# Two graph-attention layers on one core: how an aggregate's products end, and how a column of numbers becomes a row

## The chip, the cores and the metric

The kernel runs on one core of a Trainium2 chip. The core has TensorE (PE in the profile; PEld are its weight loads), VectorE (DVE), ScalarE (ACT), GpSimd (POOL) and SyncE (SP), and 16 DMA engines that move data between HBM and the on-chip memory. TensorE writes its products to PSUM, which has eight banks; DVE or ACT must copy a result out of a bank before another product may start there. The metric is the device time of one execution in microseconds (us); the times below are medians over several executions.

## The reference

There are 2708 nodes with 1024 features (`x`) and a 0/1 adjacency matrix `adj` of 2708 x 2708; all is fp32. Two layers follow each other, each with a layer norm and relu ahead of it and a residual around it:

```
h = maximum(layernorm(x), 0)                     # layer 0
f = h @ Wf + bf ;  g = h @ Wg + bg
e = relu(f @ g.T)
A = softmax(where(adj > 0, e, -9e15), axis=1)
x = x + A @ (h @ W + bW)

h = maximum(layernorm(x), 0)                     # layer 1
z = h @ W1 ;  f1 = z @ a1 ;  f2 = z @ a2
e = leaky_relu(f1 + f2.T, 0.2)
A = softmax(where(adj > 0, e, -9e15), axis=1)
x = x + relu(A @ z)
```

## The kernel before

**Tiling.** The 2708 rows are cut into 21 full tiles of 128 rows and one, TINY, of 20. Twenty full tiles form five panels (`p` = 0 to 4) and ten pairs (`pairs`, `NQ` = 10). The 21st tile (MONO) and TINY are the leftover unit: their columns are spread over panels 0 to 2, so that the panels are 576, 576, 532, 512 and 512 columns wide. Scores are held transposed: a panel is a block of columns (the rows of the reference's `A`), and all 22 tiles run through it.

**Stages.** A first phase, whose later tiles run between the score products of panel 0, normalizes `x`, transposes it, multiplies the weights `Wf` and `Wg` together and writes to DRAM what the later stages stream: `hs_d` for the scores, `hg_d` and `hgl_d` (pairs and leftovers) for the aggregates, `mk_d` for the masks. It also fills `r_`, the part of the scores that depends on one node alone; `r_` lies with 128 nodes down the partitions and a tile per column. In layer 0 each panel then goes through `scores` (score products, masks, running maximum), `column_max` and `softmax` (exponentials and their sum), `aggregate` (attention times `h`) and `project` (times `W`). Layer 1 computes its scores from two vectors (`weights1`), and goes through `aggregate` and `project` again. The stages of neighbouring panels are interleaved in the main loop (L1358 to L1387): `aggregate` of panel `p` comes after `project_q` of panel `p+1`, and `project` of panel `p` comes ahead of the scores of panel `p+1`, but for the last two panels, where the order differs. After panel 0's aggregate, background work that is left is run down (`flush`), and `spread_wa` follows.

**Strassen-Winograd.** Each large product is done with seven half-size products M1 to M7 instead of eight. `accumulate` (L554 to L585) runs them in a given order. A product accumulates over `K` steps into `NH` = 4 banks. With `by_k` set (the aggregates), the loop over the ten pairs is outside and that over the four banks inside, so that all four banks end together. M1 and M2 share the banks called x, M5 and M3 those called y, M6 and M7 those called z; M4 has its own, v. There are eight banks in all: z takes x's banks after M2, and the small products after M3 (`sum_ps`, `mx_ps`) take y's. In the profile a bank's name follows the aggregate: `gx`, `gy`, `gz`, `gv`.

**The end of a product in `aggregate`** (L788 to L880). The order is M1, M5, M2, M6, M3, M7, M4. `left` (L815) loads the left operands (`hc`, 512 KB for two pairs) when they are first asked for. M2, M3 and M4 also take in the leftover unit: `left_over` (L822) loads `hl` and multiplies MONO (L828) and then the 20 rows of TINY (L832) into the same four banks. It is called as `more[m]` after the last pair; after it come the four evictions (`evict`, L860) and one call of `behind`. M7 computes another leftover product at its middle pair (`into_m15`, banks `gw`). M2's eviction is a copy by ACT into `gT`, M3's an addition by DVE into `gT`.

**What sets the order of work.** Each engine runs its instructions in order. SP issues all loads in program order (`load`, L137), POOL issues the stores (`store`, L141), which a scheduler may move. Streamed operands share one pool of 12 buffers (`strm`), so a load can wait until an older buffer is free. `behind` runs background jobs (exponentials, masks, weight preparation) between TensorE's products at a given rate; in an aggregate it is called after pairs 2, 5 and 8 and at the end.

**From a column to a row.** The scores need `r` of a panel as a row on all partitions (`rb`). `spread` (L229) transposes one column after another on TensorE, up to four into one bank, and copies the banks out, by DVE and ACT in turn. `scores` (L1055) calls it at its start in each panel. Layer 1 spreads its own vectors in the same way. DVE and ACT instructions all carry line L45, that of a helper which records them.

Of the kernel before, what the change touches and what calls it, by code (L numbers as in the profile page):

```python
# [8 lines left out]
FP = mybir.dt.float32  # L9
# [9 lines left out]
P = 128  # L19
W = 512  # L20
# [37 lines left out]
def kernel(  # L58
# [19 lines left out]
    nc = InOrder(tc)  # L78
    N, D = x.shape
    NC = D // P  # L80
    NH = NC // 2
# [3 lines left out]
    NP = N // W  # L85
# [3 lines left out]
    width = [W + NM, W + NM, W + NY, W, W]  # L89
    base = [sum(width[:p]) for p in range(NP)]  # L90
    F = W // P
    MONO, TINY = F * NP, F * NP + 1
# [9 lines left out]
    pieces = [[(t, P) for t in full(p)] + ([(MONO, NM), (MONO, NM), (TINY, NY)][p:p + 1] if p < 3 else [])  # L102
              for p in range(NP)]
    first_col = [sum(len(q) for q in pieces[:p]) for p in range(NP)]
# [55 lines left out]
    md_d = dram.tile([P, 7, NH, W], FP, name="md_d")  # L160
    wt_d = [dram.tile([P, 4, NH, W], FP, name=f"wt{l}_d") for l in range(2)]
    mk_d = [dram.tile([P, NQ + 1, 2, width[p]], BF, name=f"mk_d{p}") for p in range(NP)]
    x1_d = [dram.tile([P if t < TINY else NY, D], FP, name=f"x1_d{t}") for t in range(NT)]

    ident = consts.tile([P, P], FP, name="ident")
# [31 lines left out]
    def behind(us, psum_free=False):  # L197
        credit[0] = min(credit[0] + us, 2 * us)
        while later and credit[0] > 0 and (psum_free or not later[0][3]) and (not later[0][4] or later[0][4]()):
            credit[0] -= one()  # L200

    def flush():
        while later:
            one()
# [24 lines left out]
    def spread(o, cols):  # L229

        at = 0
        for g in range(0, len(cols), 4):
            ps = bank("sp_ps")
            w = 0
            for cl in cols[g:g + 4]:
                n = cl.shape[0]
                nc.tensor.transpose(ps[:, w:w + n], cl.to_broadcast([n, P]), ident[:n, :n])
                w += n
            copy(o[:, at:at + w], ps[:, :w])
            at += w  # L240

    def add(o, a, b):
        nc.vector.tensor_tensor(o, a, b, OP.add)
# [4 lines left out]
    def columns_of(p, col):  # L248
        return [col[:n, i:i + 1] for i, (_, n) in enumerate(pieces[p])]
# [301 lines left out]
        picks.append(t)  # L551


    def accumulate(left, right, K, h, order, then, evict, name, prepare={}, rate=0.0, by_k=False, more={}, room=()):  # L554

        acc = {}
        at = {M1: "x", M2: "x", M5: "y", M3: "y", M6: "z", M7: "z", M4: "v" if by_k else "z"}
        for m in order:  # L560
            start = at[m] not in acc
            if start:
                acc[at[m]] = [bank(f"{name}{at[m]}{d}") for d in range(NH)]
            ps = [t[:, :h] for t in acc[at[m]]]
            for k, d in ([(k, d) for k in range(K) for d in range(NH)] if by_k else
                         [(k, d) for d in range(NH) for k in range(K)]):
                nc.tensor.matmul(ps[d], left(m, k, d), right(m, k), start=(start and k == 0),  # L567
                                 stop=(k == K - 1 and m not in more), skip_group_check=True)
                if by_k and d == NH - 1 and k % 3 == 2:
                    behind(rate)  # L570
                if by_k and d == NH - 1 and k == K // 2 and (m, k) in more:
                    more[m, k]()
                if not by_k and k == K - 1:
                    evict[m](d, ps[d])
                    behind(rate, m in room)
            if by_k:
                if m in more:
                    more[m](ps)
                for d in range(NH):
                    evict[m](d, ps[d])  # L580
                behind(rate)
            if m in prepare:
                prepare[m]()
            if m in then:
                then[m]()  # L585
# [202 lines left out]
    def aggregate(l, p, S, sm, then={}, rate=3.0):  # L788


        w = width[p]
        h = w // 2
        lo, hi = slice(0, h), slice(h, w)
        T1 = [slot("T1", (P, 2, HX)) for _ in range((NQ + 1) // 2)]
        t1 = lambda q: T1[q // 2][:, q % 2, :h]
        wa_ = lambda q: S[pairs[q][0]]
        wb_ = lambda q: S[pairs[q][1]]
        exps_until(NQ)
        for q in range(NQ):
            sub(t1(q), wa_(q)[:, hi], wa_(q)[:, lo])  # L800

        def second():
            exps_until(2 * NQ + 2 + LAG)
            for q in range(NQ):
                sub(wa_(q)[:, hi], wb_(q)[:, hi], wa_(q)[:, hi])
            for q in range(NQ):
                sub(wa_(q)[:, lo], wb_(q)[:, hi], t1(q))

        def fourth():
            for q in range(NQ):  # L810
                sub(wb_(q)[:, lo], wb_(q)[:, lo], wa_(q)[:, lo])

        hc = {}

        def left(m, q, d):  # L815
            i, j = group_of[q]
            if (m, i) not in hc:
                hc[m, i] = stream("hc", (P, 2, W))
                load(hc[m, i], hg_d[l][i][:, m])
            return hc[m, i][:, j, d * P:(d + 1) * P]  # L820

        def left_over(ps, e, s, start=False):  # L822


            two = stream("hl", (P, W + P))
            load(two, hgl_d[l][:, e])
            for d in range(NH):
                nc.tensor.matmul(ps[d], two[:, d * P:(d + 1) * P], S[MONO][:, s], start=start, stop=False,  # L828
                                 skip_group_check=True)
            for d in range(NH):  # L830
                g = slice(B32 * d, B32 * d + NY)
                nc.tensor.matmul(ps[d], two[g, W:], S[TINY][g, s], start=False, stop=True, skip_group_check=True)  # L832

        def into_m15():
            ps = [bank(f"gw{d}")[:, :h] for d in range(NH)]
            left_over(ps, 1, hi, True)
            for d in range(NH):
                add(get("m15", d), ps[d], get("m15", d))

        def right(m, q):  # L840
            if m == M5:
                return t1(q)
            s = wa_(q) if m in (M1, M6, M7) else wb_(q)
            return s[:, hi if m in (M3, M7) else lo]

        G = [None, None]
        tmp = {}
        part = lambda t, d: t[d // 2][:, d % 2, :h]

        def g(e, d, s):  # L850
            if G[0] is None:
                G[:] = both("gT")
            return G[e].rearrange("p (c i) -> p c i", c=NH)[:, d, s]

        def get(name, d):
            if name not in tmp:
                tmp[name] = in_pairs(name)
            return part(tmp[name], d)

        evict = {M1: lambda d, ps: nc.scalar.copy(get("m1", d), ps),  # L860
                 M5: lambda d, ps: add(get("m15", d), ps, get("m1", d)),
                 M2: lambda d, ps: nc.scalar.copy(g(0, d, lo), ps),
                 M6: lambda d, ps: add(get("u2", d), ps, get("m1", d)),
                 M3: lambda d, ps: add(g(0, d, hi), ps, get("u2", d)),
                 M7: lambda d, ps: (add(g(1, d, hi), ps, get("m15", d)), add(get("m1", d), ps, get("m1", d))),
                 M4: lambda d, ps: add(g(1, d, lo), ps, get("m1", d))}
        inverse = []
        of = lambda e, s: G[e].rearrange("p (c i) -> p c i", c=NH)[:, :, s]
        by = lambda s, k: inverse[0][:, s].rearrange("p (o i) -> p o i", o=1).to_broadcast([P, NH, k])

        def scale():
            for e, s, k in ((0, slice(0, w), w), (1, hi, h)):
                nc.gpsimd.tensor_tensor(of(e, s), of(e, s), by(s, k), OP.mult)  # L873

        accumulate(left, right, NQ, h, (M1, M5, M2, M6, M3, M7, M4), then, evict, "g",
                   {M5: second, M2: fourth, M3: lambda: inverse.append(inverse_sums(p, sm)), M7: scale}, rate=rate,
                   by_k=True, more={M2: lambda ps: left_over(ps, 0, lo), M3: lambda ps: left_over(ps, 0, hi),
                                    M4: lambda ps: left_over(ps, 1, lo), (M7, NQ // 2): into_m15})
        nc.vector.tensor_tensor(of(1, lo), of(1, lo), by(lo, h), OP.mult)
        return [t.rearrange("p (c i) -> p c i", c=NH) for t in G]  # L880
# [148 lines left out]
    def spread_wa():  # L1029
        for k in range(2):  # L1030
            spread(wab[k], [wa[:, k, c:c + 1] for c in range(NC)])
# [23 lines left out]
    def scores(p, B):  # L1055
# [3 lines left out]
        lo, hi = slice(0, h), slice(h, w)  # L1059
        fetch, convert, turn = makers[p]  # L1060
        rb = slot("rb")
        spread(rb, columns_of(p, r_[:, first_col[p]:]))
        acc = slot("acc")
        S = [None] * NT
        rates = (0.6, 1.0, 0.65, 0.65, 0.65)
# [294 lines left out]
    for p in range(NP):  # L1360
# [17 lines left out]
        G[p] = aggregate(0, p, S, got["sm"], then)  # L1378
        if p == 0:
            flush()  # L1380
            spread_wa()
        if p < NP - 2:
            project(0, p, G.pop(p), finish0(p), {M1: lambda p=p: first_masks(p + 1, 0),
# [126 lines left out]
```

## Time and profile before

| | |
|---|---|
| median of 4 runs | 3137.21 us (3135.26 to 3141.41) |
| the profiled execution | 3141.41 us |
| its span (first to last instruction) | 3139.3 us |
| mean granted TensorE clock | 0.989 |
| TensorE busy | 3050.6 us, 97% |
| DVE / ACT / POOL busy | 58% / 14% / 15% |
| the chain that ended last | PE 89%, DVE 4%, DMA 3% |
| data moved | 651.82 MB, 208 GB/s in the mean |

The page and the answers of the trace describe one execution. A row of the timeline or of the chain gives start (us from the start of the span), duration in us, engine, line of the kernel, the names of result and operands, and the number of instructions in the row; brackets give idle time ahead of it and what ended it. A row of the waits gives, after the colon, the total in us, the number of waits and the longest. One fp32 product appears as two instructions. `<-` stands between a result and its operands.

### The profile page before, as it was taken

Reading aid. Unit: us, or ns where it says so; the run is one execution under the profiler, and the core shown is the slowest. Engines: PE = TensorE matmul, PEld = TensorE weight load, DVE = VectorE, ACT = ScalarE, POOL = GpSimd, SP = SyncE. Lnnn points to the kernel's source line nnn. Section 1 sums busy time; section 2 is a strip of 40 time slices with the busy share of each in tenths; the row PEclk is TensorE's granted clock in tenths of the full one; section 3 lists DMA queues with packets and bytes.
Section 4 is the critical chain, followed back from the end, with each engine's and each line's share of the span. In section 5 each row is a group of like instructions: output and inputs, shape, how many; then the busy total and the mean of one; then the engine's idle time right before and its main releaser. Section 6 shows DMA issues by size and latency. Waiting matters only on the chain.

```text
span 3139.3 us, 36230 instructions
## 1 busy us (share of the span) xinstructions
PE 3050.6 (97%) x12712; PEld 2263.6 (72%) x12712; DVE 1828.6 (58%) x3730; ACT 447.2 (14%) x788; POOL 464.9 (15%) x668
## 2 busy tenths in 40 slices
PE   8978999999999999999999999998999999999998
PEld 4566777767877588876888885865757758678684
DVE  5877686286732687327872478659473571745612
ACT  3321020000200101000020002103031130311200
POOL 2653002210002110023000101021010020120202
PEclk9989999999999999999999999998999999999999
DMA  6888938878446796468955678596555565565655
GB/s 209 310 281 269 270 125 305 231 229 246 154 134 161 221 256 209 147 151 259 291 174 151 170 218 246 191 294 241 192 183 170 158 200 159 167 197 171 215 163 190
DMA packets 379109, 651.82 MB, mean 208 GB/s; under 512 B 170848, under 2 KB 211328, under 8 KB 378928
## 3 DMA queue, kind: packets, MB, share of 16 engines
q1 hardware_dynamic: 335920, 525.38, 55.4%
q0 software_dynamic: 43008, 124.13, 11.8%
q8 instruction: 101, 1.65, 0.2%
q14 instruction: 80, 0.66, 0.1%
HBM read 536.68 MB, written 112.67 MB: 207 GB/s over the span
## 4 chain that ended last, share of the span: by engine, by line
PE 89%; DVE 4%; DMA 3%; issue 1%; SPq 1%; POOL 1%; ACT 0%; DVEq 0%; POOLq 0%; ACTq 0%
PE gz L567 12%; PE gy L567 12%; PE gx L567 11%; PE sz L1077 7%; PE gv L567 6%; PE pz L969 6%; PE sx L1077 5%; PE sy L1077 5%; PE px L969 4%; PE py L969 4%; PE qz L567 3%; PE qy L567 2%; PE M_ps L483 2%; PE qx L567 2%; SPq L139 1%
## 5 line engine op out<-in xcount | busy, mean ns | idle before, releaser
L1077 PE MATMUL sz<-B,As 128*128 128x288 f32 (+2 forms) x1200 | 292.3, 393 | 8.2 <-DVE st L45 7.5
L1077 PEld LDWEIGHTS sz<-B,As 128*128 128x128 f32 x1200 | 227.4, 190 | 58.1 <-DVE st L45 11.9
L873 POOL TENSOR_TENSOR gT<-gT,rr 128x2304 f32<-128x2304 f32 (+5 forms) x20 | 72.7, 3637 | 1103.1 <-DVE rr L45 1000.0
L1077 PE MATMUL sx<-B,As 128*128 128x288 f32 (+2 forms) x800 | 201.5, 395 | 13.1 <-DMA As<-hs_d 12.2
L1077 PE MATMUL sy<-B,As 128*128 128x288 f32 (+2 forms) x800 | 199.0, 392 | 0.0
L567 PE MATMUL gz<-P,hc 128*128 128x288 f32 (+2 forms) x800 | 186.0, 393 | 2.3 <-ACT gT L45 2.3
L567 PE MATMUL gz<-Sa,hc 128*128 128x288 f32 (+2 forms) x800 | 186.0, 393 | 2.3 <-ACT gT L45 2.3
L567 PE MATMUL gx<-P,hc 128*128 128x288 f32 (+2 forms) x800 | 186.8, 395 | 0.1
L1077 PEld LDWEIGHTS sx<-B,As 128*128 128x128 f32 x800 | 152.4, 191 | 44.9 <-DMA As<-hs_d 12.7
L567 PE MATMUL gy<-T,hc 128*128 128x288 f32 (+2 forms) x800 | 184.2, 391 | 0.0
L567 PEld LDWEIGHTS gx<-P,hc 128*128 128x128 f32 x800 | 153.5, 192 | 33.2 <-issue 1.9
L567 PEld LDWEIGHTS gz<-Sa,hc 128*128 128x128 f32 x800 | 151.2, 190 | 36.0 <-ACT gT L45 4.4
L567 PEld LDWEIGHTS gz<-P,hc 128*128 128x128 f32 x800 | 150.9, 190 | 35.7 <-ACT gT L45 4.5
L567 PEld LDWEIGHTS gy<-T,hc 128*128 128x128 f32 x800 | 152.0, 190 | 30.5
L1077 PEld LDWEIGHTS sy<-B,As 128*128 128x128 f32 x800 | 151.7, 190 | 30.6 <-DVE st L45 0.3
L969 PE MATMUL pz<-w,ps 128*128 128x512 f32 x320 | 142.1, 594 | 0.8 <-DVE pt L45 0.8
L969 PE MATMUL py<-w,ps 128*128 128x512 f32 x320 | 142.2, 594 | 0.0
L969 PE MATMUL px<-w,gT 128*128 128x512 f32 x320 | 141.8, 595 | 0.0
L143 POOL DMA_DIRECT2D out_dram<-x_res x180 | 89.2, 502 | 265.0 <-DVE x_res L45 242.6
L45 DVE TENSOR_TENSOR gT<-gy,u 128x288 f32<-128x288 f32 (+2 forms) x40 | 14.8, 432 | 183.5 <-PE gy L832 183.5
L45 DVE TENSOR_TENSOR u<-gz,m 128x288 f32<-128x288 f32 (+2 forms) x40 | 17.6, 440 | 170.9 <-PE gz L567 170.5
L143 POOL DMA_DIRECT2D mk_d<-mask x55 | 36.0, 655 | 541.4 <-DVE mask L45 518.2
(318 smaller groups left out, 5092.3 us busy)
## 6 DMA issues: line engine op xcount, KB each, us to landing
hc<-hg_d SPq DMA_DIRECT2D x350, 512.0 KB, 3.9
As<-hs_d SPq DMA_DIRECT2D x150, 512.0 KB, 5.4
w<-wt_d SPq DMA_DIRECT2D x96, 512.0 KB, 5.2
w<-in_L_gnn_W_dram SPq DMA_DIRECT2D x72, 512.0 KB, 4.1
md<-md_d SPq DMA_DIRECT2D x56, 512.0 KB, 4.4
adj_i<-in_adj_dram SPq DMA_DIRECT2D x200, 128.0 KB, 4.8
hs_d<-hsT POOLq DMA_DIRECT2D x40, 512.0 KB, 4.7
hg_d<-g POOLq DMA_DIRECT2D x36, 512.0 KB, 5.0
```

The costliest lines, as they stand in the source:

```text
L45: i = f(*a, **k)
L139: tc.keep_in_program_order(nc.sync.dma_start(a, b))
L143: nc.gpsimd.dma_start(a, b)
L483: nc.tensor.matmul(ps, wfT[a][c // NH][:, c % NH, :], wgT[b][c], start=(c == 0), stop=(c == NC - 1))
L567: nc.tensor.matmul(ps[d], left(m, k, d), right(m, k), start=(start and k == 0), stop=(k == K - 1 and m not in more), skip_group_check=True)
L873: nc.gpsimd.tensor_tensor(of(e, s), of(e, s), by(s, k), OP.mult)
L969: nc.tensor.matmul(ps, left[i][m][:, k, :], w_[k], start=(start and k == 0), stop=(k == NH - 1), skip_group_check=True)
L1077: nc.tensor.matmul(ps[:n, :h], lefts[q][:, i % 2, c, :n], B[m][c // 2][:, c % 2, :h], start=(start and c == 0), stop=(c == NH - 1), skip_g ...
```

## The change

It has two parts.

*How the aggregates' products end.* With `by_k`, only pairs 0 to 7 (`whole` = K - TAIL = 8) keep the interleaved order. Then come the leftover products, for M2, M3 and M4, and then, bank by bank, pairs 8 and 9 and at once that bank's eviction. This holds for all seven products. `behind` is called after pairs 2, 5 and 7 and at the end. The flag that closes an accumulation moves from the leftovers to the last pair.

*r by DMA.* For panels 1 to 4, `columns_to_row` writes the columns of `r_` into a row in DRAM (`r_d`), after panel 0's aggregate in the program: one POOL transfer of 128 x 4 single elements for each panel, and one of 64 or 20 elements for panels 1 and 2. `scores` then loads the row onto all partitions with one SP transfer (`row_on_all`). Panel 0 and layer 1 spread by TensorE as before. In the compiled program the six stores stand in the first phase: the short ones next to the last `hg_d` stores near 123 us of the profile before, the others where that profile is at about 199 us (two), 244 us and 290 us. The four loads of `rb` stand on SP behind the last `w` loads of the projection before and ahead of the panel's first `adj_i` and `As` loads; that of panel 4 stands behind the last `hc` of panel 3's aggregate.

On SP, the `hl` load of M2, M3 and M4 moves ahead of the last `hc` load of the same product.

```diff
+    r_d = [dram.tile([1, WX], FP, name=f"r_d{p}") for p in range(NP)]
...
+    def columns_to_row(row, p, col):
+        k = len(pieces[p])
+        nc.gpsimd.dma_start(row[0:1, :W].rearrange("o (i p) -> p (o i)", p=P), col[:, :F])
+        if k > F:
+            n = pieces[p][F][1]
+            nc.gpsimd.dma_start(row[0:1, W:W + n].rearrange("o n -> n o"), col[:n, F:k])
+
+    def row_on_all(o, row, p, by=load):
+        by(o[:, :width[p]], row[0:1, :width[p]].to_broadcast([P, width[p]]))
...
+    TAIL = 2
...
-            for k, d in ([(k, d) for k in range(K) for d in range(NH)] if by_k else
-                         [(k, d) for d in range(NH) for k in range(K)]):
-                nc.tensor.matmul(ps[d], left(m, k, d), right(m, k), start=(start and k == 0),
-                                 stop=(k == K - 1 and m not in more), skip_group_check=True)
-                if by_k and d == NH - 1 and k % 3 == 2:
+            whole = K - TAIL
+            for k, d in ([(k, d) for k in range(whole) for d in range(NH)] + [(k, d) for d in range(NH) for k in range(whole, K)]
+                         if by_k else [(k, d) for d in range(NH) for k in range(K)]):
+                nc.tensor.matmul(ps[d], left(m, k, d), right(m, k), start=(start and k == 0), stop=(k == K - 1),
+                                 skip_group_check=True)
+                if by_k and d == NH - 1 and k < whole and (k % 3 == 2 or k == whole - 1):
                     behind(rate)
                 if by_k and d == NH - 1 and k == K // 2 and (m, k) in more:
                     more[m, k]()
-                if not by_k and k == K - 1:
+                if by_k and d == NH - 1 and k == whole - 1 and m in more:
+                    more[m](ps)
+                if k == K - 1:
                     evict[m](d, ps[d])
-                    behind(rate, m in room)
+                    if not by_k:
+                        behind(rate, m in room)
             if by_k:
-                if m in more:
-                    more[m](ps)
-                for d in range(NH):
-                    evict[m](d, ps[d])
                 behind(rate)
...
-                nc.tensor.matmul(ps[d], two[g, W:], S[TINY][g, s], start=False, stop=True, skip_group_check=True)
+                nc.tensor.matmul(ps[d], two[g, W:], S[TINY][g, s], start=False, stop=start, skip_group_check=True)
...
-        spread(rb, columns_of(p, r_[:, first_col[p]:]))
+        if p == 0:
+            spread(rb, columns_of(p, r_[:, first_col[p]:]))
+        else:
+            row_on_all(rb, r_d[p], p)
...
         if p == 0:
             flush()
+            for s in range(1, NP):
+                columns_to_row(r_d[s], s, r_[:, first_col[s]:])
             spread_wa()
```

## The prediction, made before the changed kernel ran

> **What bounds the kernel now.** I read the busy table first, then the waits of TensorE, then the chain and the timeline of one aggregate, then POOL and SP where the change puts transfers. From the page of the kernel before:
> ```profile
> PE 3050.6 (97%) x12712; PEld 2263.6 (72%) x12712; DVE 1828.6 (58%) x3730; ACT 447.2 (14%) x788; POOL 464.9 (15%) x668
> ```
> TensorE (PE) is busy for 3050.6 of 3139.3 us; 89 us remain, and any change must come out of these or out of the instructions. TensorE's waits:
> ```profile
> PE sum_ps L771 <- DVE gT L45: 5.1, 10, 0.5
> ...
> PE gz L567 <- ACT gT L45: 4.6, 10, 0.5
> PE gx L567 <- DMA hc<-hg_d: 3.9, 1, 3.9
> ```
> The columns are the total in us, the number of waits and the longest. Ten aggregates (five panels, two layers) each wait twice for an eviction of `gT`: 9.7 us. The third line is one wait for a load. The chain through one aggregate (layer 1, panel 1) shows how both kinds stand on the path:
> ```profile
> 2418.20 0.73 PE gx L832 x8
> 2418.93 0.39 ACT gT L45
> 2419.32 0.04 issue
> 2419.36 19.67 PE gz L567 x80
> ...
> 2460.37 0.73 PE gy L832 x8
> 2461.11 0.45 DVE gT L45
> 2461.55 0.04 issue
> 2461.60 1.24 PE sum_ps L771 x4
> ```
> After the leftover products (L828, L832) nothing is left to run on TensorE while the first bank is copied out, and the next product (`gz`, M6) takes that very bank. A product shows as two instructions, so x80 are 40 products: 19.40 us (`gy`), 0.485 us each; `gz` took 0.27 more on restarting.
>
> **What the Trainium skill says.** "Perfetto Trace Analysis", Matmuls: independent groups should rotate through PSUM banks, so that one's evacuation overlaps the next's matmuls. The trace agrees: the projections (L969), whose products end one bank at a time, wait 0.8 us on an eviction in the whole span; the aggregates, which end with all four banks at once, 9.7. "DMA: Bandwidth & Descriptors", Rules for kernel authors: a strided last dimension lowers to one descriptor per element; the kernel before shows no DMA of 512 single elements. The same page, Anatomy of one DMA, fits about 2.0 us and a bandwidth term for a POOL transfer; the trace has 2.7 us to landing for the 64x1 `r<-r` and 4.7 for 512 KB `hs_d`. "TensorE: Matmul & The Clock Gate", Part 4, puts a transpose at about 275 ns in context for bf16; here an fp32 one lasts 272 ns at the median, and five overlap to 0.80 us.
>
> **Part 1, the ends of M2, M3, M4.** Pairs 0 to 7 stay interleaved over banks, then come the leftovers, then each bank gets pairs 8 and 9 and is evicted. Instructions and operands are the same. The first bank now ends three banks' work before the last: 3 x 2 x 0.485 = 2.9 us, against 0.39 us (ACT, M2) and 0.45 us (DVE, M3) for its eviction. M6 needs the fourth bank only at its fourth product, 3 x 0.485 = 1.46 us in, against the same 0.4. So both waits go.
> M2 to M6 before: 0.73 (L832) + 0.39 + 0.04 + 19.67 = 20.83 us. After: 0.70 + 0.20 + 19.40 = 20.30. The 0.20 is the step from a 20-row group to full rows: after the `gw` leftovers, 32 instructions took 7.96 us instead of 32 x 0.2425 = 7.76. Gain 0.53.
> M3 to `sum_ps` before: 0.73 + 0.45 + 0.04 + 1.24 = 2.46. After: 0.70 + 0.20 + 0.97 (4 instructions of 0.2425) = 1.87. Gain 0.59.
> M4 to the projection: no wait now,
> ```profile
> 2508.42 0.77 PE L832 MATMUL gv<-P,hl 20*128 20x288 f32 x8
> 2509.12 6.28 PE L969 MATMUL px<-w,gT 128*128 128x512 f32 x14
> ```
> (timeline, whose durations include the last one's drain), so 0.
> Sum 1.12 x 10 = 11.2 us; the waits alone give 9.7. Below that only if the evictions are not free to run at once. DVE works in order and is 58% busy; that it now gets four evictions spaced by 0.97 us instead of a burst leaves it 0.5 us of room in each space. M1, M5, M6 and M7 now also end inside this order (the last two pairs bank by bank, all seven products): M7 to M4 waits on evictions only in layer 1's panels 0 and 1 (`gv` 19.67 for 19.40); 2 x 0.2 = 0.4 us.
> The leftovers need the weights of the last two tiles 3.9 us earlier. In layer 1's panel 0 the last exponential ends at 2203.6 and M2's leftovers would come at 2212.7, so that cover holds with 9 us.
> The background work (`behind`) is called after pairs 2, 5, 7 instead of 2, 5, 8: DVE gets the same work 2 us earlier, at no cost.
>
> **Part 2, loads that trade places on SP.** SP issues in the order written. The leftovers' `hl` load moves ahead of the last `hc` of each of the three products. Where loads run ahead that costs nothing. Where they don't is panel 0 of layer 0:
> ```profile
> 505.27 2.59 SPq L139 DMA_DIRECT2D hc<-hg_d  x2
> ...
> 509.88 0.33 SPq L139 DMA_DIRECT2D hl<-hgl_d  x1
> ```
> (SP's timeline) and, on TensorE's,
> ```profile
> 511.44 9.72 PE L567 MATMUL gx<-Sb,hc 128*128 128x288 f32 x32 [3.89 <-DMA hc<-hg_d]
> ```
> The `hc` of pairs 6, 7, issued at 505.27, had waited for a stream buffer that a store of an earlier `w_rows` still held; it lands at 511.4 and TensorE stalls 3.89 us. In the new order a 512 KB `w_rows` load takes over that wait, directly ahead of this `hc`; behind it come two more `w_rows`, `hl`, and then `hc` of pairs 8, 9, about when `hl` was issued (509.88). At 310 GB/s, the fastest slice of the page, 512 KB take 1.7 us; part of it runs beside the `hc`: +1 us. Ends: -1 (`hc` follows closely, with nothing else of its own to wait for) and +3 (it moves wholly behind, at the slower rate of a crowded queue). A second stall isn't due: pairs 8, 9 are needed 3.9 + 2.7 us after the restart at about 512, and a load issued near 510 takes 3.9 to land.
>
> **Part 3, r by DMA.** In panels 1 to 4 the transposes of `r` (5, 5, 4, 4) and six copies go; panel 0 and all of layer 1 keep theirs. In exchange POOL issues six stores once in the first phase, and SP four broadcast loads, each after the projection's `w` loads and ahead of the panel's `adj_i` and `As`.
> The spreads stand between projections and scores (panel 3's):
> ```profile
> 1454.89 0.60 PE L237 MATMUL sp_ps<-ident,r 128*128 128x128 f32 x4
> ```
> Start to start they take 0.73 (panel 1), 0.69, 0.44 and 0.48 us. Panel 3 waits 0.67 us for DVE soon after, so its 0.44 is taken back there: 0.73 + 0.69 + 0.48 = 1.9 us. Ends: 0 (the scores' later waits on DVE, 0.9 us in panel 1 and 2.0 in panel 2, absorb what TensorE gains) and 2.8 (DVE's copies also gone). Broadcast loads wait only on slots long free; at 3 to 5 us to landing they are hidden by the projections of some 80 us.
> POOL: an issue of 128 rows takes 0.54 us, one of 128x2 0.72, so 1.4 ns per further descriptor; 512 elements come to 1.1 us. The four fall at 199, 199, 244 and 290 us, two before an idle stretch of 12.1, one in that of 5.7 ahead of 246.78, one in that of 5.10 ahead of 292.38:
> ```profile
> 254.06 0.55 POOL L143 DMA_DIRECT2D hg_d<-x  x1 [4.24 <-ACT x L45]
> ```
> So 0. If that cover is gone (first scores at about 270 us already wait 12.2 for `As`, whose chain starts at this 254.06), each us costs 1 us.
>
> **Sum.** -11.2 - 0.4 + 1 - 1.9 = -12.5. On the profiled span 3139.3 gives 3126.8, with the 2.1 us around it 3128.9 for the profiled execution's 3141.41. That execution is the slowest of four; on their median 3137.21 the forecast is 3124.7, a factor of 0.996. No change means within 0.2% (6.3 us), about what a measurement of this kernel can tell.
>
> **Rivals.** *Half the gain (3130, chance 0.20).* The eviction waits go, but spreads give 0, and panel 0's load stall costs +3, and a third of the 11.2 is lost where M2's ACT copies queue behind an exponential of 0.68 us: -11.2 + 3.7 + 3 = about -5 to -7. For it: the loads trade places in a stretch that already stalls. Against: only one of 30 tails shows a wait for a load.
> *The waits stay (3136, chance 0.07).* If M6's first product waits for the last of the four evictions and not for its own bank's, the bank order hides nothing, since the last bank still ends with the aggregate's last product: M6 would wait 0.4 as before. For it: all ten waits are named `gT` without a bank. Against: 0.39 is just one copy, and four in a row on ACT would take 1.6. Only part 3 and the 0.4 remain.
> *Slower (3145, chance 0.05).* The element-wise stores hold POOL far longer than 1.4 ns per element. The one at 244 has 4.24 us of idle time after it and about 2.5 before: 6.7 us of room. To cancel 12.5 it must hold POOL for 19.2 us, 37 ns per element; beyond that `hg_d` and with it the first `As` come late by the rest, 27 us (53 ns) giving 3145. For it: no such DMA in the trace. Against: 1.4 ns from two rows of the same queue.
> *More (3119, chance 0.08).* The panel 0 load comes earlier and takes its 3.9 us stall away.
>
> **How the numbers follow.** The forecast has 0.60, its own range 3121 to 3129 (part 1 from -9.7 to -11.6, the load -1 to +3, spreads 0 to -2.8, sampling of the median 1.5). Over all cases 3118 to 3133 leaves out the unchanged and the slow case, and a little on the other side. Faster by over 0.2% means below 3130.9: 0.60 + 0.08 + about 0.17 of the half-gain case. Within 0.2%: the rest of it and the waits that stay, 0.10. Slower 0.05.
>
> **What would show it.** Right: the two lines `gT` vanish from TensorE's waits; TensorE's busy time falls by 2 to 6 us; after L832 the next rows are `gx<-..,hc` with no bracket, and `gz` follows at once; no `sp_ps<-ident,r` after panel 0; POOL's rows to `r_d` last about 1 us. Wrong: a new wait of the ten M6 starts on ACT or DVE; `gx <- DMA hc` over 7 us; the first `sx <- DMA As` above 12.2; rows to `r_d` of ten us or more, which would make the kernel slower.

## The result, and the profile after

The changed kernel takes 3135.52 us (median of 33 runs, 3128.30 to 3141.77), the kernel before 3139.01 (53 runs). The ratio is 0.999, with a 95% interval of 0.9985 to 0.9995: some 3.5 us faster, between 1.6 and 4.7, where 12.5 were forecast. That lies outside the range given (3118 to 3133), and by the bound of 0.2% it counts as no change. The profiled execution of the changed kernel took 3132.08 us.

The ends of the aggregates did what was said. In TensorE's waits of the changed kernel the two lines with `gT` are gone; what stands there instead, from that view (total us, number, longest):
```profile
PE sx L1094 <- DMA As<-hs_d: 13.0, 2, 9.1
...
PE gx L582 <- DMA hc<-hg_d: 4.8, 1, 4.8
...
PE sz L1094 <- DMA As<-hs_d: 3.3, 1, 3.3
```
Before, `As` was waited for once:
```profile
PE sx L1077 <- DMA As<-hs_d: 12.2, 1, 12.2
```
Now there are three waits with 16.3 us in sum, and the one for `hc` grew from 3.9 to 4.8.

The chain of the changed kernel through the same aggregate (layer 1, panel 1):
```profile
2408.38 0.70 PE gx L846 x8
2409.07 4.08 PE gx L582 x16
2413.15 19.40 PE gz L582 x80
...
2450.01 0.70 PE gy L846 x8
2450.71 4.08 PE gy L582 x16
2454.79 0.97 PE sum_ps L785 x4
```
No ACT and no DVE piece stands between products any more. 4.08 is 16 x 0.2425 plus the step of 0.20; `gz` takes 19.40 instead of 19.67, `sum_ps` 0.97 instead of 1.24. All this is as worked out.

To find the rest I laid the starts of the same products in both timelines side by side. The changed kernel loses or gains in few places (before less after, us): about 3.4 gained by 180 us, of which 2 to 2.7 by 40 us, ahead of the first instruction that differs, and so chance; 5.6 lost between 284 and 309; 1.6 net lost in panel 0's M2; then 0.53 to 0.61 gained at each later end, and 0.77, 0.79, 0.54 and 0.49 at the four spreads, of which panel 3's 0.54 is given back at once. The loss of 5.6 is this stall on TensorE, with the slow products after it, new in the changed kernel's timeline:
```profile
307.48 2.76 PE L1094 MATMUL sx<-B,As 128*128 128x288 f32 x6 [3.83 <-DMA As<-hs_d]
```
`As` reads `hs_d`, which POOL stores. POOL's timeline of the changed kernel ahead of the stall, with the element-wise store of panel 4's `r` (L246):
```profile
287.36 0.76 POOL L246 DMA_DIRECT2D r_d<-r  x1 [3.41 <-DVE r L45]
```
Its issue takes 0.76 us, less than the 1.1 estimated, and the next store on POOL waits for DVE, not for it. But here are the DMA issues from 284 to 306 us of the changed kernel (KB each, median us to landing):
```profile
hs_d<-hsT POOLq DMA_DIRECT2D x3, 512.0 KB, 12.5
...
r_d<-r POOLq DMA_DIRECT2D x1, 2.0 KB, 12.0
```
and from 288 to 310 us of the kernel before:
```profile
hs_d<-hsT POOLq DMA_DIRECT2D x3, 512.0 KB, 7.4
```
2 KB take 12.0 us to land, and the 512 KB stores that follow take 12.5 instead of 7.4. The same in data moved: five us of the changed kernel behind that store, then five us at the same place of the kernel before (the last two numbers are the DMA engines' share and GB/s):
```profile
294.00:299.00 5.00, 5.00 (x22) 3.92 (x21) 3.85 (x9) 0.00 (x0) 0.00 (x0) 1.00 0.78 63
```
```profile
298.00:303.00 5.00, 5.00 (x23) 3.90 (x22) 3.23 (x7) 0.00 (x0) 0.00 (x0) 1.00 0.97 324
```
The stalled `As` did not wait for these `hs_d` stores, though: SP has no wait for `hs_d` in this stretch. The way from the store to `As` leads over SP. In front of `As` stand four `adj_t` loads of 16 KB, and the issue of the first alone takes 11.71 us; once `As` is issued, it lands in 4.5 us. The chain of the changed kernel, then these four loads on SP in the changed kernel and, at the same place, in the kernel before (where the longest of them takes 6.23 us):
```profile
289.54 11.71 SPq L139
...
302.84 4.50 DMA As<-hs_d
```
```profile
289.54 13.13 SPq L139 DMA_DIRECT2D adj_t<-in_adj_dram  x4
```
```profile
293.50 7.64 SPq L139 DMA_DIRECT2D adj_t<-in_adj_dram  x4
```
So the theory (A): the stores of single elements choke the transfers of the whole core for about 10 us each, and two of the four stand where the first scores run out of loaded operands soon after. (The expectations below put the path through the late `hs_d` stores; the late stores are a sign of the choke, and the path to TensorE is that of SP's loads.) Rivals: (B) the gain of the ends is lost in the loads that trade places on SP, whatever `r` does; (C) the first phase differs by chance.

### The profile page after: what moved, and what is told of

It reads as the page before. It is cut to its first block, busy times and chain, and to the rows that moved or that the text cites. A ratio compares the mean times of both kernels' runs of the same rounds, so it can differ in the third digit from the quotient of the medians.

```text
span 3130.3 us, 36210 instructions
## 1 busy us (share of the span) xinstructions
PE 3047.7 (97%) x12694; PEld 2262.3 (72%) x12694; DVE 1831.9 (59%) x3727; ACT 449.6 (14%) x785; POOL 469.5 (15%) x674
## 4 chain that ended last, share of the span: by engine, by line
PE 85%; DVE 4%; DMA 4%; issue 3%; SPq 2%; POOL 1%; ACT 0%; DVEq 0%; POOLq 0%; ACTq 0%
PE gy L582 12%; PE gz L582 12%; PE gx L582 12%; PE sz L1094 6%; PE pz L983 6%; PE gv L582 5%; PE sx L1094 4%; PE sy L1094 4%; PE px L983 4%; PE py L983 4%; PE qz L582 3%; PE qy L582 2%; PE qx L582 2%; PE M_ps L495 2%; SPq L139 2%
## 5 line engine op out<-in xcount | busy, mean ns | idle before, releaser
L983 PEld LDWEIGHTS pz<-w,ps 128*128 128x128 f32 x320 | 60.2, 190 | 77.1 <-issue 70.5
```

Source lines behind the costliest of these rows:

```text
L983: nc.tensor.matmul(ps, left[i][m][:, k, :], w_[k], start=(start and k == 0), stop=(k == NH - 1), skip_group_check=True)
```

## The experiments

All times are medians; each kernel ran beside the kernel before on the same chip, which took 3138.80 to 3139.57 us.

**The two parts apart.** The first kernel has the new ends alone:
```diff
-        if p == 0:
-            spread(rb, columns_of(p, r_[:, first_col[p]:]))
-        else:
-            row_on_all(rb, r_d[p], p)
+        spread(rb, columns_of(p, r_[:, first_col[p]:]))
...
-            for s in range(1, NP):
-                columns_to_row(r_d[s], s, r_[:, first_col[s]:])
```


> The changed kernel with all spreads of r by TensorE again: no r_d stores, no rb loads; only the new ends of the aggregates' products. Theory A (the element-wise r_d stores crowd the DMA engines in the first phase; hs_d stores behind them land late, and with them As): the first phase is that of the kernel before; -11.2 from the ends and +1.6 from panel 0's load leave about 3129 us, ratio to before 0.997, some 6 us below the changed kernel. Theory B (the gain of the ends is lost in loads that trade places, whatever r does): about the time of the changed kernel, 3135. Theory C (the first phase differs by chance from execution to execution): 3129 to 3135, and the stall of 3.8 us ahead of the scores' products near 307 us shows here too.

Measured: 3128.19 us, ratio 0.9964 (0.9951 to 0.9976), 11.1 us faster than before. The waits at 258 and 307 us are gone; the one of 12.2 us stands as before.

The second has `r` by DMA alone: `accumulate` as in the kernel before, the rest as changed.

> The kernel before with only r by DMA. Theory A: slower than before, by 5.6 (stall after the stores of 241 and 287 us) - 1.9 (spreads gone) = about 4 us: 3143, with new waits for As near 260 and 307 us. Theories B and C: -1.9, about 3137.

Measured: 3148.01 us, ratio 1.0025 (1.0015 to 1.0034): 8.7 us slower, more than the 4 expected. TensorE's timeline of this kernel:
```profile
263.30 4.18 PE L1094 MATMUL sz<-B,As 128*128 128x288 f32 x8 [3.56 <-DMA As<-hs_d]
275.77 3.89 PE L1094 MATMUL sx<-B,As 128*128 128x288 f32 x8 [5.55 <-DMA As<-hs_d]
303.93 4.21 PE L1094 MATMUL sx<-B,As 128*128 128x288 f32 x8 [10.88 <-DMA As<-hs_d]
```
These waits come to 20.0 us for 12.2 before. Here the last `As` was issued 1.2 us after the store at 290.36 us, and itself took 12.31 us to land. B falls (the ends keep their gain without `r`), and so does C: the stalls come and go with the stores.

**The stores later.** The six stores are kept in program order, after panel 0's aggregate (both in `columns_to_row`):
```diff
-        nc.gpsimd.dma_start(row[0:1, :W].rearrange("o (i p) -> p (o i)", p=P), col[:, :F])
+        tc.keep_in_program_order(nc.gpsimd.dma_start(row[0:1, :W].rearrange("o (i p) -> p (o i)", p=P), col[:, :F]))
```


> The changed kernel with the six r_d stores kept in program order, so that POOL issues them after panel 0's aggregate (about 610 us). Theory A: the loss of the first phase goes; if the stores do as little harm there as DMA traffic allows, about 3127; up to 3133 if the four stores of 10 to 12 us hold up the loads of panel 0's projection instead. Theory B and C: no change, 3135.

Measured: 3144.85 us, ratio 1.0016 (1.0010 to 1.0023), slower than either expectation. The first phase is clean, but the stores are now four in a row at 595 to 599 us. Two stretches of this kernel behind them, and what TensorE then waits for:
```profile
596.00:606.00 10.00, 10.00 (x43) 7.85 (x42) 0.00 (x0) 0.00 (x0) 5.37 (x8) 1.00 0.59 49
606.00:616.00 10.00, 10.00 (x56) 7.65 (x55) 2.90 (x6) 0.59 (x1) 2.55 (x3) 1.00 0.36 26
```
```profile
638.32 8.92 PE L983 MATMUL py<-w,ps 128*128 128x512 f32 x16 [8.40 <-DMA w<-wt_d]
```
For 20 us the core moves 49 and 26 GB/s, where the changed kernel has 174 and 220. `w` is loaded by SP: its loads, not only POOL's stores, come late: SP is held by the loads in front of them and issues the first `w` at 632.6 us, for 616.0 in the changed kernel. And the DMA engines show a share of 0.36 in the worst stretch: they are not shown busy while little arrives.

**The number of pieces, at the same places and the same 2 KB.** Each partition writes its four values side by side (the row is then in another order, and the scores of panels 1 to 4 are not those of the reference):
```diff
-        nc.gpsimd.dma_start(row[0:1, :W].rearrange("o (i p) -> p (o i)", p=P), col[:, :F])
+        nc.gpsimd.dma_start(row[0:1, :W].rearrange("o (p i) -> p (o i)", p=P), col[:, :F])
```


> The changed kernel with the four large r_d stores at the same places and of the same 2 KB, but each partition writes its four values side by side: 128 pieces of 16 bytes in place of 512 of 4. The row in r_d, and so what the scores add for panels 1 to 4, is in another order: this part of the computation is changed. Theory A1 (the time that a store holds the DMA engines goes with its number of pieces): landing of about 4 us instead of 10 to 12, hs_d stores behind it back near 5 us, no stall at 307 us; about 3128. Theory A2 (any store on POOL's queue between those of hs_d does it, by its place in the order): landing and stalls as before, 3135.

Measured: 3128.22 us, ratio 0.9964 (0.9950 to 0.9978), 7.3 us below the changed kernel. From 284 to 306 us of this kernel:
```profile
hs_d<-hsT POOLq DMA_DIRECT2D x4, 512.0 KB, 6.8
...
r_d<-r POOLq DMA_DIRECT2D x1, 2.0 KB, 6.6
```
The store lands in 6.6 us for 12.0, `hs_d` in 6.8 for 12.5, and no wait stands at 307. So A2 falls: it is how the store is cut, not its place on the queue. But A1 isn't shown by this run, for number and size of the pieces changed together, and in the changed kernel the stores of 64 and of 20 elements landed as late (11.0 and 10.1 us) as those of 512 (8.3 to 12.0). Four more runs, below, take this apart.

**Which of the four stores.** First `r` by DMA for panels 1 and 2 alone, then for panels 3 and 4 alone; the other panels spread by TensorE:
```diff
-            for s in range(1, NP):
+            for s in (1, 2):          # second kernel: (3, 4)
...
-        if p == 0:
+        if p not in (1, 2):           # second kernel: (3, 4)
```


> The changed kernel with r by DMA for panels 1 and 2 alone; panels 3 and 4 spread by TensorE, so that the stores near 241 and 287 us are gone and those near 120 and 196 us stay. If the loss comes from stores between those of hs_d that the first scores wait for (theory A): the waits near 258 and 307 us go, about 3127.5. If every element-wise store costs alike, wherever it stands: half of the loss stays, about 3131.

> The complement of the run with panels 1 and 2: r by DMA for panels 3 and 4 alone, so that only the element-wise stores near 241 and 287 us remain. Theory A (the stores between those of hs_d do the harm): nearly the whole loss of the changed kernel, 3134 to 3137, with the stalls near 258 and 307 us. If each of the four stores costs alike: about 3131.5.

Measured: 3127.91 us (ratio 0.9965, 0.9953 to 0.9978) with the stores for panels 1 and 2, 3142.25 us (1.0008, 1.0000 to 1.0016) with those for 3 and 4. The first two choke the transfers too. The next transfers behind the stores at 199 us are issued from 206.6 us on (until then little is asked for, in the kernel before as well). In the first kernel, issued between 206 and 212 us:
```profile
hg_d<-g POOLq DMA_DIRECT2D x2, 512.0 KB, 8.4
```
and in the kernel before, between 203 and 213 us:
```profile
hg_d<-g POOLq DMA_DIRECT2D x2, 512.0 KB, 3.6
```
With these stores and an `As` load under way the core moves 2 and then 7 GB/s, for two us each from 206.6 us on. But TensorE is busy throughout: its operands had been loaded. In the second kernel it waits soon after the store at 289 us:
```profile
302.89 3.97 PE L1094 MATMUL sx<-B,As 128*128 128x288 f32 x8 [11.12 <-DMA As<-hs_d]
```
It loses 14 us against the ends alone, and the full change, with the same two stores, 7 us. The two profiles show what the store happened to hold up on SP: in the changed kernel an `adj_t` load that TensorE did not need yet (3.83 us of waiting), here the next `As` itself (12 us to land, 11.12 of waiting). Why one kernel meets the worse case and the other does not is not settled; the runs of the changed kernel alone spread over 13 us.

**What about these stores chokes the transfers.** Four kernels with the new ends alone, and nothing but the two stores of panels 3 and 4 added at their places, unread. The target is the row (`row[0:1, ...]`) for the first two:
```diff
+        nc.gpsimd.dma_start(row[0:1, :W].rearrange("o (i p) -> p (o i)", p=P), col[:, :F])   # f0
...
+        nc.gpsimd.dma_start(row[0:1, :P].rearrange("o p -> p o"), col[:, F - 1:F])           # f1
...
+        nc.gpsimd.dma_start(row.rearrange("(i p) w -> p i w", p=P)[:, :, 0:1], col[:, :F].rearrange("p (i o) -> p i o", o=1))   # f2: rows of 512 bytes
...
+        nc.gpsimd.dma_start(row[:, :, :F], col[:, :F].rearrange("p (o i) -> p o i", o=1).to_broadcast([P, F, F]))   # f3: 16 bytes of every 32
```


> The ends alone (r by TensorE), and only the two element-wise stores of panels 3 and 4 added, at the same places (near 241 and 287 us); nothing reads what they write. Control for the three kernels that follow. If the stores alone choke the transfers: 3142, as with r by DMA for panels 3 and 4, with waits of about 11 us for As near 303 us, landing 10 to 12 us. If the rb loads had a part in it: nearer to 3128.

> The same two stores with one column instead of four: 128 pieces of 4 bytes. If the time goes with the number of pieces: landing of 3 to 4 us, 3128 to 3130. If it goes with the size of a piece, whatever their number (in the changed kernel the stores of 64 and of 20 elements landed in 10 to 11 us too): landing of 10 us and 3140 to 3142.

> The same two stores of 512 pieces of 4 bytes, but each piece goes to a row of its own, 512 bytes from the next. If pieces of four bytes wait for each other because they fall side by side in memory: landing near 5 us and about 3128 to 3130. If a small piece is slow wherever it goes: as the control, 3142.

> The same two stores with 512 pieces of 16 bytes, 16 bytes apart. If the number of pieces decides: as the control, 3142, or slower. If the four bytes decide: as with the 128 pieces of 16 bytes, landing of 4 to 7 us and about 3128.

| | pieces | bytes each | next piece | landing of the two, us | time, us | ratio to before |
|---|---|---|---|---|---|---|
| f0 | 512 | 4 | adjoins | 10.1, 12.4 | 3140.30 | 1.0000 (0.9991 to 1.0008) |
| f1 | 128 | 4 | adjoins | 7.0, 10.1 | 3136.39 | 0.9990 (0.9983 to 0.9997) |
| f2 | 512 | 4 | 512 bytes on | 3.5, 6.4 | 3131.62 | 0.9975 (0.9965 to 0.9984) |
| f3 | 512 | 16 | 32 bytes on | 3.5, 7.0 | 3130.37 | 0.9971 (0.9960 to 0.9982) |

The control f0 loses what the stores lose elsewhere, without any `rb` load. A quarter of the pieces (f1) still costs 8 us more than the ends alone, where f0 costs 12, so the harm does not go in proportion to the number. 512 pieces of the same four bytes cause no such stall once they lie apart: TensorE's timeline of f2 has only the waits that the ends alone have there,
```profile
259.63 2.21 PE L1084 MATMUL sz<-B,As 128*128 128x288 f32 x8 [0.60 <-DVE st L45]
276.34 4.21 PE L1084 MATMUL sx<-B,As 128*128 128x288 f32 x8 [12.56 <-DMA As<-hs_d]
```
where f1's has
```profile
258.86 2.18 PE L1084 MATMUL sz<-B,As 128*128 128x288 f32 x8 [1.78 <-DMA As<-hs_d]
273.46 3.74 PE L1084 MATMUL sx<-B,As 128*128 128x288 f32 x8 [10.49 <-DMA As<-hs_d]
307.17 3.87 PE L1084 MATMUL sx<-B,As 128*128 128x288 f32 x8 [3.00 <-DMA As<-hs_d]
```
SP shows the same: the longest issue of an `adj_t` load between 286 and 306 us takes 11.0 us in f0 and 10.3 in f1, but 3.3 in f2 and 4.5 in f3. The medians of f2 and f3 still lie 3.4 and 2.2 us above the ends alone; the intervals overlap, so whether a small cost is left is open. So A1 falls as I had put it: what chokes is pieces of four bytes written side by side in memory. The Trainium skill, "DMA: Bandwidth & Descriptors", Specifications, says that transfers under 512 bytes are done as read-modify-write. That neighbouring pieces then wait for each other would fit, but is argued, not shown; and the adjoining pieces of 16 bytes, which are under 512 too, landed in 4.0 to 6.6 us.

**The row another way.** One transpose of all of `r_`, one copy, one store of 23 rows of 512 bytes; `rb` is loaded from it as before:
```diff
+        nc.tensor.transpose(ps[:n, :P], cols, ident)
+        copy(t, ps[:n, :P])
+        tc.keep_in_program_order(nc.gpsimd.dma_start(rows, t))
```


> The changed kernel with the six element-wise stores replaced by one transpose of all of r on TensorE after panel 0's aggregate, one copy, and one store of 23 rows of 512 bytes; the rb loads stay. Theory A: -11.2 -0.4 -1.9 +1.6 +0.3 (transpose) = about 3127.5, at or below the kernel with late stores, without any stall near 260 or 307 us. Theory B and C: 3135.

Measured: 3135.13 us, ratio 0.9987 (0.9981 to 0.9994). The waits at 258 and 307 us are gone, but my edit made another, on POOL, whose timeline for this kernel has
```profile
616.04 0.54 POOL L250 DMA_DIRECT2D r_d<-rT  x1 [20.01 <-DVE rT L45]
622.30 7.13 POOL L1323 DMA_DIRECT2D x_res<-in_L_gnn_bW_dram  x8 [5.72 <-PE px L986]
```
POOL stands 20 us in front of the store, for the transpose, and the `x_res` transfers that the changed kernel issues at 592 to 611 us queue behind it. DVE then gets them late and TensorE waits for DVE (1.7 and 0.9 us in the projection, 2.0 in the scores). With the same three lines at the end of panel 0's scores:

> As the kernel with one transpose and one store of 23 rows, but placed at the end of panel 0's scores (about 410 us), so that the store on POOL stands ahead of nothing that is waited for. The run with the late place lost 20 us of POOL's time in front of the x_res loads of panel 0's projection; if that is all that cost it, this one gives 3128.2 (the ends alone) - 1.9 + 0.3 = about 3126.6. If the rb loads themselves cost something, or the spreads hid nothing, 3128 or more.

Measured: 3130.86 us, ratio 0.9974 (0.9964 to 0.9984). It doesn't beat the ends alone (3128.19). In the traces the spreads' gain is there (2.2 us between 521 and 1772 us), but not in the sum; differences of 2 to 3 us are within these intervals.

**Panel 0's loads.** With the ends alone, TensorE waits in M2 of panel 0 (its timeline):
```profile
508.26 5.84 PE L582 MATMUL gx<-Sb,hc 128*128 128x288 f32 x16 [4.16 <-DMA hc<-hg_d]
515.04 2.21 PE L842 MATMUL gx<-Sa,hl 128*128 128x288 f32 x8 [0.95 <-DMA hl<-hgl_d]
```
Together 5.1 us, 1.2 more than the 3.89 before. In the twelve traces that have the new ends with two last pairs and the preparation of W in its old place, these waits range from 3.7 to 6.9 us with 5.8 in the middle, so that +1.9 is nearer than the +1 of the prediction. Two kernels ask whose it is. In the first, one pair instead of two ends bank by bank (`TAIL = 1`), which gives SP the order of the kernel before:

> The ends alone (r by TensorE), with one last pair bank by bank instead of two. The first bank then ends 1.46 us ahead of the last, still more than the 0.39 and 0.45 us of an eviction, so the 11.2 us stay; and the hl load falls back behind the last hc, so that SP's order is that of the kernel before. If trading these loads costs 1.2 us, as the profile of the ends alone has it (stalls of 4.2 and 0.9 us for 3.9): about 3127. If the ends need the longer cover, more than 3129.

Measured: 3131.74 us, ratio 0.9974 (0.9964 to 0.9984), worse than expected. Its timeline shows why:
```profile
520.54 3.64 PE L842 MATMUL gx<-Sa,hl 128*128 128x288 f32 x8 [3.87 <-DMA hl<-hgl_d]
```
`hl` now comes last from SP, but is needed a pair earlier than in the kernel before: 2.62 for `hc` and 3.87 for `hl` make 6.5 us. What counts is not the order alone but each load's distance from its use. In the second, the preparation of W, whose `w_rows` loads stand among these, starts one product later:
```diff
-        then = {M5: prepare_W} if p == 0 else {}
+        then = {M2: prepare_W} if p == 0 else {}
```


> The ends alone (r by TensorE), and the preparation of W in panel 0's aggregate starts after M2 instead of after M5, so that no w_rows load stands between the hc loads of M2. If panel 0's stall of 4.2 us (and 0.9 for hl) is owed to these loads, it goes, and the kernel takes about 3123.5; if the stall only moves to M6 or M3, or the preparation is late at the end of the aggregate, 3127 to 3130.

Measured: 3120.41 us, ratio 0.9942 (0.9929 to 0.9954): 7.8 us below the ends alone, 18.4 below the kernel before on this chip (3138.80). The timeline of M2:
```profile
492.23 15.68 PE L582 MATMUL gx<-Sb,hc 128*128 128x288 f32 x64
507.75 2.10 PE L842 MATMUL gx<-Sa,hl 128*128 128x288 f32 x8
```
No wait is left, and none has moved to M6 or M3. The gain is more than the 5.1 us in the profile of the ends alone; 5.8, the middle of the twelve, leaves 2 us that are within these intervals.

**All that helped.** The later preparation with the early transpose, and with one last pair:

> Everything that helped, with r by one transpose: the ends, the later preparation of W, and r stored as 23 rows of 512 bytes at the end of panel 0's scores. If what r by DMA saves in the four spreads (1.9 - 0.3) reaches the end: 3120.4 - 1.6 = 3118.8. If the spreads were hidden, or the rb loads cost as much as they save: 3120.4 or more.

> The ends with one last pair, r by TensorE, and the later preparation of W. With that there is no load left that a trade on SP could make late, so no difference to the same with two last pairs: 3120.4, within 1 us.

Measured: 3121.64 (ratio 0.9943, 0.9931 to 0.9956) and 3120.63 us (0.9940, 0.9926 to 0.9954). `r` by DMA adds nothing that can be measured, even well done; and with the loads out of the way one last pair covers an eviction as well as two. The simplest of the best versions is the new ends, the spreads on TensorE and the later preparation: 3120.4 us.

## Why the prediction was wrong

- *Part 1, the ends: right.* -11.2 and -0.4 forecast; the ends alone gave -11.1 by the medians, with +1.2 of panel 0's load in it, and 0.53 to 0.61 at each end by the traces. The rivals on this part (the waits stay; ACT busy with an exponential) didn't come.
- *Part 2, loads that trade places: right in sign, sized low.* +1 forecast; +1.2 with the ends alone, +1.9 in the middle of twelve traces, 2.1 lost by M2 in the changed kernel's profile, all inside the bounds given. In five of the twelve `hl`, which the new order needs first, is waited for too (0.6 to 1.0 us); the prediction looked for a second stall only at the last `hc`.
- *Part 3, the spreads: right in the trace, not seen in the medians.* 1.9 forecast; 0.77 + 0.79 + 0.49, with panel 3's 0.54 given back, make 2.05.
- *Part 3, POOL: this step failed.* "512 elements come to 1.1 us ... So 0." The issue takes 0.76 us, as cheap as said. But the step priced the stores only where they are issued, and looked for cover in POOL's idle stretches. It left out what happens after the issue: 8 to 12 us to landing, in which the core's other transfers slow to a fraction (63 GB/s for 324) and SP's loads for the first scores are held. The term was put at 0. By the medians the full change is 7.3 us slower than the ends alone; with the 2 us that the spreads give, about 9 us is what the stores cost (an estimate from these two). The one landing it named, 2.7 us for a 64x1 transfer that stays inside on-chip memory, was not carried into the sum, and no bound from above was set. The rule quoted there, of one descriptor per element, pointed at the number of pieces, which f1 to f3 show is not what decides.
- *The slower rival* named the right instructions and the right victim (`As`), but the wrong carrier: it asked that POOL be held for 19.2 us, so that `hg_d` and with it `As` come late. POOL is held for 0.76 us; what is held is the transfers under way and SP. Asked of these, the two stores at 244 and 290 us would have been the ones to look at, for TensorE soon needs what they hold up; behind those at 199 us it had its operands.

## What to carry to other kernels

A DMA has a price in three places: its issue, its landing, and what it takes from transfers under way; a column written element by element into a row of DRAM was cheap in the first alone. If it must be made, let each piece be 16 bytes or more (128 adjoining ones did no harm here), or turn the column first and store whole rows; or put it where nothing is about to be loaded. Where a stage already waits for loads, look for others among them that can start later: one word moved here was worth twice what the whole change brought.

## What the runs showed of the hardware that I had not expected

- A store of 512 adjoining pieces of four bytes (2 KB) takes about 0.8 us to issue and 8.3 to 12.4 us to land (10.4 to 18.0 with four of them in a row); 64 or 20 such pieces land no sooner (9.2 to 11.2). The same 512 pieces laid 512 bytes apart land in 3.5 and 6.4 us, 128 adjoining pieces of 16 bytes in 4.0 to 6.6, 512 of 16 in 3.5 and 7.0.
- While the adjoining ones are under way, the core's other transfers nearly stand, those of SP too: 2 and 7 GB/s for two us each behind two such stores, 49 and 26 GB/s for ten us each behind four of them and two shorter ones. Two short ones alone do it: from 127 to 131 us the changed kernel moves 79 GB/s behind its 64 and 20 pieces, the ends alone 381. Even the issue of one 16 KB load on SP took 10.3 to 11.7 us in three kernels. In these stretches the DMA engines' share reads 0.02 to 0.78, so a low share was no sign of free engines.
